# A tree layer's matmuls in another order, and an alignment's planned lengths

## The chip, the core and the metric

The kernel runs on one core of a Trainium2 chip. The metric is the device time of one execution in microseconds, as the median of several runs. The profile comes from one further execution.

## The reference

A decoder of four layers works on 64 sequences of 64 tokens with 128 features, and a context of the same shape. Each layer adds an attention, a cross part and a feed-forward part to the tokens `x`. Two parts of the first layer matter here.

The cross part of the first layer is an alignment: for each sequence, the distances between its context rows and its tokens, the cheapest path through the 64x64 table, found by running sums over rows and then followed back, and the context rows added to the tokens along that path.

The feed-forward part of the first layer has three decision trees (`q`, `k`, `v`) of 16 leaves. Each token falls into one leaf of each tree and goes through that leaf's small two-layer network; then tokens attend to each other inside a sequence:

```python
sel = one_hot(leaf, 16)
hidden_all = relu(einsum('nd,ldh->lnh', xf, w1) + b1[:, None, :])
hidden = hidden_all * sel.T[:, :, None]
out = einsum('lnh,lho->no', hidden, w2) + sel @ b2
```

## The kernel before

The 4096 tokens form 8 blocks of 512. The work is written as small parts. A part has a name, a function that issues its instructions, the engines that may run it with a planned length on each, the parts it must follow, and the buffers it takes and frees. `Flow.add` (line 124) collects parts. `Flow.search` (223) plays the list many times with random priorities, from planned lengths alone, and keeps the shortest play. `Flow.run` (263) then issues the parts in that order and fixes the order of instructions on every engine (`Pinned`, 66). There are three such plans: for the first layer (`L0_group`, 1183), for the second (`L1_group`), and for the third and fourth together (`L2_group`, 2303).

Every engine works through its own list in order, so a part that waits holds up what stands behind it on that engine. SP issues almost all loads and stores, also in order: first inputs and weights, then the zeroing of large DRAM buffers (lines 2300 and 1910), then the trees' weights (1493, 1495), then what the parts ask for.

The parts of the first layer, in the names that the text uses:

- Attention, per block: normalization (`bn`, `rs`, `xn`), transposes, keys and queries, key masks `m0` to `m3` (405 on VectorE, 403 on ScalarE), four score parts (466, 16 rows in the trace each), their row maxima (487) and subtractions (496) on VectorE, exponentials (501), transposes and their evictions (1063, 517), value parts (531), divisions (557 to 562), then a norm per head, whose sums are on VectorE (620, 632) and whose power and scaling are on GpSimd (1074, 639), projection and residual (664, 667).
- Distances, per block: a load of the context rows (1307, 1309), the part `aa` on ScalarE, which squares them (1314), products (1334, 1335), inverses and a Newton step on VectorE (1345 to 1351), and a store to DRAM.
- Alignment, for blocks 0 to 2 and for blocks 3 to 7: one load of the distances; parts `c0` to `c15` on VectorE, each four rows of running sums (1392, 1393); then per chunk of eight rows `k` (1413 to 1415) and `l` (1421 to 1423), which make masks, and `t15` down to `t0`, each four rows of the way back (1433 to 1438); then one store, and per block the path part: loads (1466, 1468), a product (1473) and an addition (1476).
- Trees, per block: decision `dc` on VectorE (1530 to 1548), a transpose of the choice and its evictions `lo` (1554 to 1563), which also makes the bf16 tile `notT` that is 1 for each leaf that was not chosen. For each of three trees, eight chunks of two leaves, taken in pairs: `u` (1565) makes a pair's hidden values in a two-bank PSUM buffer, `r` (1577) adds the bias and applies relu, one half after the other, mostly on ScalarE (1583), and `d` (1588) multiplies by the second weights (1599; for the third tree 1609, with the 16-row product 1611 for the leaves' biases). Then scores, a softmax and the sum of values.

A chunk of `u` has two matmuls into one PSUM bank. The large product (1573) multiplies the 128 features with a chunk's weights in float32, which the trace shows as two passes of 512 columns. The small one (1574) has 16 rows of bf16: it adds a huge negative number to the hidden values of all leaves that a token did not choose, so that relu makes them zero. Large and small products alternate: chunk 0 large, chunk 0 small, chunk 1 large, chunk 1 small. There are two such PSUM buffers for `u` and for the attention's scores together.

Of the kernel before, what the change touches and what calls it, by code (L numbers as in the profile page):

```python
# [24 lines left out]
S = 64  # L25
# [30 lines left out]
CH = 8  # L56
# [47 lines left out]
class Flow:  # L104
# [19 lines left out]
    def add(self, key, on, f, after=(), takes=(), frees=(), shift=0.0, late=False, tail=0.0):  # L124


        assert key not in self.keys, key
        self.keys.add(key)
        ring = lambda n: RING.get(n, n)
        need = {}  # L130
        for n, _, _ in takes:
            r = ring(n)
            k, room = need.get(r, (0, 0))
            need[r] = k + 1, max(room, k + 1, ROOM.get(n, 0))
        self.wait.append((key, on, f, tuple(k for k in after if k is not None), [(ring(n), n, t, u) for n, t, u in takes],
                          [(ring(n), t) for n, t in frees], shift, late, tail, [(r, k, room) for r, (k, room) in need.items()]))
# [832 lines left out]
class Decoder:  # L969
# [321 lines left out]
    def flow_L0_xattn(self, fl, blks, p0, x):  # L1291

        nc, g = self.nc, blks[0]
# [78 lines left out]
        def add(name, on, f, after=(), takes=(), frees=(), tail=0.0):  # L1372
            fl.add(G(name), on, f, after=[G(a) if isinstance(a, str) else a for a in after],
                   takes=[(r, G(t), u) for r, t, u in takes], frees=[(r, G(t)) for r, t in frees], tail=tail)
# [29 lines left out]
        def least(c):  # L1404
            def f(e):
                t = self.sb("mk", (P, CH * (3 * S + 1)), BF16)
                du = t[:, 0 : CH * 2 * S].rearrange("p (i a j) -> p i a j", a=2, j=S)
                lf = t[:, CH * 2 * S :].rearrange("p (i j) -> p i j", j=S + 1)
                mk[c] = du, lf
                a, b = slice(CH * c, CH * c + CH), slice(CH * c + 1, CH * c + CH + 1)  # L1410
                cd, cu, cl = r[sl, a, 0:S], r[sl, a, 1 : S + 1], r[sl, b, 0:S]
                mn = self.sb("mn", (P, CH, S))
                nc.vector.tensor_tensor(mn[sl], cu, cl, ALU.min)
                nc.vector.tensor_tensor(du[sl, :, 0], cd, mn[sl], ALU.is_le)
                nc.vector.tensor_tensor(du[sl, :, 1], cu, cl, ALU.is_le)
            return f

        def back(c):
            def f(e):
                du, lf = mk[c]  # L1420
                nc.vector.memset(lf[sl, :, S : S + 1], 0.0)
                nc.vector.scalar_tensor_tensor(du[sl, :, 1], du[sl, :, 0], 0.5, du[sl, :, 1], ALU.is_lt, ALU.mult)
                nc.vector.scalar_tensor_tensor(lf[sl, :, 0:S], du[sl, :, 0], 0.5, du[sl, :, 1], ALU.is_lt, ALU.subtract)
            return f

        def trace(k):

            def f(e):
                for i in range(4 * k + 3, 4 * k - 1, -1):
                    src = self.dt_en  # L1430
                    if i < S - 1:
                        st = self.dt_st
                        nc.vector.tensor_tensor(
                            st[sl, :, 0:S], self.bc(r[sl, i + 2 : i + 3, 1:], [n8, 2, S]), mk[(i + 1) // CH][0][sl, (i + 1) % CH], ALU.mult,
                        )
                        src = self.dt2.tile([P, S], F32, name="m")
                        nc.vector.tensor_tensor(src[sl], st[sl, 0, 1 : S + 1], st[sl, 1, 0:S], ALU.add)
                    nc.vector.tensor_tensor_scan(
                        r[sl, i + 1, 1:][:, ::-1], mk[i // CH][1][sl, i % CH, 1 : S + 1][:, ::-1], src[sl, ::-1], 0.0, ALU.mult, ALU.add,
                    )  # L1440
            return f

        per = CH // 4
        for c in range(S // CH - 1, -1, -1):
            add(f"k{c}", {"DVE": 1.8}, least(c), [f"k{c+1}"] if c < S // CH - 1 else [f"c{S//4-1}"],
                [("mk", f"m{c}", per + (c > 0)), ("mn", f"n{c}", 1)], [("mn", f"n{c}")])
            add(f"l{c}", {"DVE": 1.3}, back(c), [f"k{c}"])
            for k in range(per * c + per - 1, per * c - 1, -1):
                first = k == per * c + per - 1 and c < S // CH - 1
                add(f"t{k}", {"DVE": 3.0}, trace(k), [f"l{c}"] + ([f"t{k+1}"] if k < S // 4 - 1 else []), [],  # L1450
                    [("mk", f"m{c}")] + ([("mk", f"m{c+1}")] if first else []))

        def store(e):
# [54 lines left out]
    def flow_L0_ffn(self, fl, blk, x):  # L1508
        nc, one, c = self.nc, self.f0, self.c
        w1, w2, em, b2 = self.f0_w1, self.f0_w2, self.f0_em, self.f0_b2  # L1510
        st, xb = {}, self.x[blk]
        add, K = self.adder(fl, "L0_ffn", blk)
# [52 lines left out]
        def up(m, pr):  # L1565
            k = slice(32 * m, 32 * m + 16)

            def f(e):
                st["hT", m, pr] = self.sb("hT", (P, 2, BT))
                ps = st["up", m, pr] = self.pair()  # L1570
                for i in range(2):
                    ch = 2 * pr + i
                    nc.tensor.matmul(ps[:, i], w1[:, m, ch, :], st["xT"], start=True, stop=False)  # L1573
                    nc.tensor.matmul(ps[:, i], em[k, ch, :], st["notT"][k], start=False, stop=True)  # L1574
            return f

        def relu(m, pr):
            def f(e):
                ps, hT = st.pop(("up", m, pr)), st["hT", m, pr]
                for i in range(2):  # L1580
                    b = self.f0_b1[:, m, 2 * pr + i : 2 * pr + i + 1]
                    if e is nc.scalar:
                        nc.scalar.activation(hT[:, i], ps[:, i], AF.Relu, bias=b)  # L1583
                    else:
                        nc.vector.tensor_scalar(hT[:, i], ps[:, i], b, 0.0, ALU.add, ALU.max)
            return f

        def down(m, pr):
            k = slice(32 * m, 32 * m + 16)

            def f(e):
                if pr == 0:
                    st["dn", m] = self.acc([P, BT])
                    st["o", m] = self.sb("va" if m == 2 else "qk")
                ps, hT = st["dn", m], st.pop(("hT", m, pr))
                last = pr == 3
                if m < 2:
                    for i in range(2):
                        nc.tensor.matmul(ps, w2[:, m, 2 * pr + i, :], hT[:, i], start=(pr + i == 0), stop=False)  # L1599
                    if last:  # L1600
                        nc.tensor.matmul(ps, b2[k, :], st["selT"][k], start=False, stop=True)
                else:
                    if pr == 0:

                        nc.tensor.matmul(ps, self.onesb[0:1, :], em[0:1, 1:5, :].rearrange("p c f -> p (c f)"), start=True, stop=False)
                    for t in range(TB):
                        tok = slice(t * P, (t + 1) * P)
                        for i in range(2):
                            nc.tensor.matmul(ps[:, tok], hT[:, i, tok], w2[:, m, 2 * pr + i, :], start=False, stop=False)  # L1609
                        if last:  # L1610
                            nc.tensor.matmul(ps[:, tok], st["selT"][k, tok], b2[k, :], start=False, stop=t == TB - 1)
            return f
# [54 lines left out]
        add("lo", {"ACT": 1.15, "DVE": 1.35}, leaves_out, ["lv"], [], [("tp", "lv")])  # L1667
        for m in range(3):
            for pr in range(4):
                add(f"u{m}{pr}", {"PE": 2.15}, up(m, pr), ["xT", "lo"] + ([f"u{m}{pr-1}"] if pr else []), [("mm", f"u{m}{pr}", 1), ("hT", f"h{m}{pr}", 1)] + ([] if pr else [("dnq", f"d{m}", 1)]),  # L1670
                    [("xT", "xT"), ("nT", "nT")])
                add(f"r{m}{pr}", {"ACT": 1.4, "DVE": 1.5}, relu(m, pr), [f"u{m}{pr}"], [], [("mm", f"u{m}{pr}")])
                add(f"d{m}{pr}", {"PE": 1.75 + (pr == 3) * (.86 if m < 2 else .5)}, down(m, pr),
                    [f"r{m}{pr}"] + ([f"d{m}{pr-1}"] if pr else []),
                    [] if pr else [("av", f"d{m}", 1), ("va" if m == 2 else "qk", f"o{m}", 1)],
                    [("hT", f"h{m}{pr}")] + ([("selT", "selT")] if pr == 3 else []))
            add(f"o{m}", {"ACT": .65, "DVE": .72} if m else {"ACT": .65}, out(m), [f"d{m}3"], [], [("av", f"d{m}"), ("dnq", f"d{m}")])
# [909 lines left out]
```

## Time and profile before

| what | us |
|---|---|
| median of 3 runs | 2339.93 (2337.36 to 2343.73) |
| the profiled execution | 2339.11 |
| its span | 2336.9 |
| TensorE busy | 2002.4 |
| VectorE busy | 1335.8 |
| ScalarE busy | 1088.6 |
| GpSimd busy | 833.2 |
| line 1573, large products, 384 rows | 213.3 |
| line 1574, small products, 192 rows | 74.0 |

The span runs from the first to the last instruction of the core, so 2.2 us of the execution lie around it. The mean granted TensorE clock was 0.904. A row such as "x384" counts passes: a float32 matmul shows as two. Ends of matmuls are modelled and overlap the next start, so the start of one matmul to the start of the next says what it took. In the rows of waits, the columns are who waited, for whom, the sum, the number of times and the longest. In a timeline, the columns are start, length, engine, line, operation and tiles, shapes, and how many alike were merged.

### The profile page before, as it was taken

Reading aid. Unit: us, or ns where it says so; the run is one execution under the profiler, and the core shown is the slowest. Engines: PE = TensorE matmul, PEld = TensorE weight load, DVE = VectorE, ACT = ScalarE, POOL = GpSimd, SP = SyncE. Lnnn points to the kernel's source line nnn. Section 1 sums busy time; section 2 is a strip of 40 time slices with the busy share of each in tenths; the row PEclk is TensorE's granted clock in tenths of the full one; section 3 lists DMA queues with packets and bytes.
Section 4 is the critical chain, followed back from the end, with each engine's and each line's share of the span. In section 5 each row is a group of like instructions: output and inputs, shape, how many; then the busy total and the mean of one; then the engine's idle time right before and its main releaser. Section 6 shows DMA issues by size and latency. Waiting matters only on the chain.

```text
span 2336.9 us, 42116 instructions
## 1 busy us (share of the span) xinstructions
PE 2002.4 (86%) x16746; PEld 1296.9 (55%) x16746; DVE 1335.8 (57%) x3680; ACT 1088.6 (47%) x2111; POOL 833.2 (36%) x1157
## 2 busy tenths in 40 slices
PE   7570959999999999979699994899999998983995
PEld 4450643445353457756476762566776765662763
DVE  8489887974020027967712333878978776871121
ACT  6560433233232347755323332666757765651432
POOL 7410460002000016453721116862235334143776
PEclk9785569999999999988799995899999999986998
DMA  9310021011000000000224441100000000012543
GB/s 255 94 37 5 19 71 23 1 25 27 0 1 0 1 10 2 15 27 16 64 74 132 139 156 44 33 10 2 6 6 25 2 6 20 6 37 79 93 80 29
DMA packets 146769, 97.78 MB, mean 42 GB/s; under 512 B 36477, under 2 KB 137646, under 8 KB 146318
## 3 DMA queue, kind: packets, MB, share of 16 engines
q1 hardware_dynamic: 125598, 63.39, 10.5%
q0 software_dynamic: 20976, 31.72, 5.7%
q8 instruction: 132, 2.16, 0.4%
q14 instruction: 63, 0.52, 0.1%
HBM read 58.67 MB, written 36.40 MB: 41 GB/s over the span
## 4 chain that ended last, share of the span: by engine, by line
PE 57%; DVE 17%; POOL 13%; issue 5%; DMA 4%; SPq 3%; ACT 1%; POOLq 0%; DVEq 0%; ACTq 0%
PE mm L1573 8%; PE ps L1063 6%; PE ps L1599 5%; PE ps L531 5%; POOL out_x L2396 4%; PE mm L466 4%; PE mm L2020 4%; PE ps L2028 3%; PE ps L1609 3%; PE mm L1574 3%; DVE e L487 3%; DVE B L496 2%; POOL moe_x L834 2%; PE ps L421 2%; DMA out_x<-ye,to 2%
## 5 line engine op out<-in xcount | busy, mean ns | idle before, releaser
L466 PE MATMUL mm<-K,G 32*64 32x256 f32 x2560 | 175.3, 414 | 86.1 <-DVE B L496 82.6
L517 ACT COPY B<-ps 128x512 f32<-128x512 f32 x320 | 178.4, 587 | 116.4 <-PE ps L1063 115.3
L1583 ACT ACTIVATE H<-mm,f_b 128x512 f32<-128x512 f32 x182 | 115.2, 684 | 245.8 <-PE mm L1574 245.8
L501 ACT ACTIVATE B<-B 128x1024 f32<-128x1024 f32 x160 | 168.3, 1058 | 117.1 <-DVE B L496 116.0
L1573 PE MATMUL mm<-G,w 128*128 128x512 f32 x384 | 213.3, 638 | 0.0
L487 DVE TENSOR_REDUCE e<-mm 128x16 f32<-128x1024 f32 x160 | 193.4, 1216 | 29.8 <-PE mm L466 28.2
L531 PE MATMUL ps<-vx,B 128*64 128x18 f32 (+1 forms) x5120 | 182.5, 219 | 32.6 <-ACT B L517 26.9
L1063 PE MATMUL ps<-cpack,B 128*128 128x128 f32 x1280 | 196.6, 294 | 11.6 <-ACT B L517 5.7
L531 PEld LDWEIGHTS ps<-vx,B 128*64 128x64 f32 x5120 | 169.3, 143 | 66.3 <-ACT B L517 32.9
L496 DVE TENSOR_TENSOR B<-mm,e 128x1024 f32<-128x1024 f32 x160 | 192.4, 1215 | 3.5 <-PE ps L1063 0.7
L1063 PEld LDWEIGHTS ps<-cpack,B 128*128 128x128 f32 x1280 | 152.9, 149 | 60.4 <-issue 29.0
L1073 POOL TENSOR_SCALAR rs_t<-ln_mv 128x4 f32<-128x4 f32 x88 | 17.5, 199 | 470.1 <-DVE ln_mv L1144 426.9
L466 PEld LDWEIGHTS mm<-K,G 32*64 32x64 f32 x2560 | 83.7, 139 | 145.8 <-issue 100.0
L1063 PE MATMUL ps<-cpack,G 128*128 128x128 f32 x544 | 98.4, 304 | 68.4 <-ACT G L1164 30.5
L2396 POOL DMA_INDIRECT out_x<-ye,to x80 | 125.1, 1564 | 52.5 <-DVE ye L2394 28.2
L1631 DVE TENSOR_TENSOR G<-ps,cpack 128x512 f32<-128x512 f32 x8 | 5.5, 686 | 236.2 <-PE ps L1628 236.1
L1063 PEld LDWEIGHTS ps<-cpack,G 128*128 128x128 f32 x544 | 67.5, 151 | 104.6 <-ACT G L1164 39.2
L1164 ACT ACTIVATE G<-x,ln_sh,ln_rs 128x128 f32<-128x128 f32 x224 | 92.1, 485 | 66.1 <-POOL ln_sh L1158 66.1
L1599 PE MATMUL ps<-H,w 128*128 128x512 f32 x256 | 120.6, 608 | 0.0
L2021 ACT ACTIVATE hT<-mm,w 128x512 f32<-128x512 f32 x92 | 63.2, 687 | 121.7 <-PE mm L2020 106.4
L1574 PEld LDWEIGHTS <-f_em 16*128 16x128 bf16 x192 | 17.4, 90 | 146.7 <-issue 146.7
L2384 ACT ACTIVATE hT<-mm,f_b 128x512 f32<-128x512 f32 (+1 forms) x96 | 58.9, 616 | 84.0 <-PE mm L2383 83.5
(424 smaller groups left out, 4255.1 us busy)
## 6 DMA issues: line engine op xcount, KB each, us to landing
xe<-pages SPq DMA_DIRECT2D x23, 264.0 KB
paged<-ye SPq DMA_DIRECT2D x23, 256.0 KB, 2.4
pages<-z SPq DMA_DIRECT2D x11, 528.0 KB, 10.2
moe_x<-z SPq DMA_DIRECT2D x8, 660.0 KB, 9.2
xe<-moe_x SPq DMA_DIRECT2D x8, 660.0 KB
G<-in_ctx SPq DMA_DIRECT2D x16, 256.0 KB, 3.1
ctxT<-in_ctxT SPq DMA_DIRECT2D x2, 2048.0 KB, 9.1
w<-in_L_ffn_w SPq DMA_DIRECT2D x16, 256.0 KB, 3.3
```

The source lines that it names most:

```text
L466: nc.tensor.matmul(sc[b * S : (b + 1) * S, gi, pr * 256 : (pr + 1) * 256], qT[rows, at : at + S], kx[rows, :, at : at + S], start=self.bia ...
L487: nc.vector.tensor_reduce(mx, sc.rearrange("p g (r k) -> p (g r) k", k=S), AX.X, ALU.max)
L496: nc.vector.tensor_tensor(ex, sv, d.bc(st["mx", u].unsqueeze(2), [P, 16, S]), ALU.subtract)
L501: nc.scalar.activation(st["ex", u], st["ex", u], AF.Exp)
L517: (nc.scalar.copy if e is nc.scalar else nc.vector.tensor_copy)(st["pT", u][:, gi], st.pop(("pt", u, gi)))
L531: nc.tensor.matmul(av[b * S : (b + 1) * S, pr, 2 * gi + jp], pT[:, gi, 2 * pr + jp, b * S : (b + 1) * S], v[:, (2 * dp + pr) * 2 + b, 2 * ...
L1063: self.nc.tensor.transpose(t[:cols, i, :], src[:, i, :], self.ident)
L1573: nc.tensor.matmul(ps[:, i], w1[:, m, ch, :], st["xT"], start=True, stop=False)
L1583: nc.scalar.activation(hT[:, i], ps[:, i], AF.Relu, bias=b)
L1599: nc.tensor.matmul(ps, w2[:, m, 2 * pr + i, :], hT[:, i], start=(pr + i == 0), stop=False)
L2020: nc.tensor.matmul(ps, w[:, ch * P : (ch + 1) * P], q["xT"], start=True, stop=True)
L2396: d = nc.gpsimd.indirect_dma_start(self.out[:, :], bass.IndirectOffsetOnAxis(ap=to[:, r0 + i : r0 + i + 1], axis=0), ye[:, r0 + i, :], Non ...
```

## The change

In `u`, a pair has both large products first and both small ones after them; before, each chunk had its large and its small product together. The number of matmuls, their operands and their PSUM banks are the same.

Four planned lengths change: those of the alignment's parts `k`, `l` and `t` on VectorE, and that of `u` on TensorE. The instructions of these parts are the same apart from the order inside `u`; the plan of the first layer is searched with the new lengths.

```diff
-            add(f"k{c}", {"DVE": 1.8}, least(c), [f"k{c+1}"] if c < S // CH - 1 else [f"c{S//4-1}"],
+            add(f"k{c}", {"DVE": 2.1}, least(c), [f"k{c+1}"] if c < S // CH - 1 else [f"c{S//4-1}"],
                 [("mk", f"m{c}", per + (c > 0)), ("mn", f"n{c}", 1)], [("mn", f"n{c}")])
-            add(f"l{c}", {"DVE": 1.3}, back(c), [f"k{c}"])
+            add(f"l{c}", {"DVE": 1.75}, back(c), [f"k{c}"])
...
-                add(f"t{k}", {"DVE": 3.0}, trace(k), [f"l{c}"] + ([f"t{k+1}"] if k < S // 4 - 1 else []), [],
+                add(f"t{k}", {"DVE": 3.35}, trace(k), [f"l{c}"] + ([f"t{k+1}"] if k < S // 4 - 1 else []), [],
...
                 for i in range(2):
-                    ch = 2 * pr + i
-                    nc.tensor.matmul(ps[:, i], w1[:, m, ch, :], st["xT"], start=True, stop=False)
-                    nc.tensor.matmul(ps[:, i], em[k, ch, :], st["notT"][k], start=False, stop=True)
+                    nc.tensor.matmul(ps[:, i], w1[:, m, 2 * pr + i, :], st["xT"], start=True, stop=False)
+                for i in range(2):
+                    nc.tensor.matmul(ps[:, i], em[k, 2 * pr + i, :], st["notT"][k], start=False, stop=True)
...
-                add(f"u{m}{pr}", {"PE": 2.15}, up(m, pr), ["xT", "lo"] + ([f"u{m}{pr-1}"] if pr else []), [("mm", f"u{m}{pr}", 1), ("hT", f"h{m}{pr}", 1)] + ([] if pr else [("dnq", f"d{m}", 1)]),
+                add(f"u{m}{pr}", {"PE": 2.35}, up(m, pr), ["xT", "lo"] + ([f"u{m}{pr-1}"] if pr else []), [("mm", f"u{m}{pr}", 1), ("hT", f"h{m}{pr}", 1)] + ([] if pr else [("dnq", f"d{m}", 1)]),
```

## The prediction

> **What bounds the kernel now.** I read the busy rows by slice first, to find where the two edited layers lie.
>
> ```profile
> PE   7570959999999999979699994899999998983995
> DVE  8489887974020027967712333878978776871121
> PEclk9785569999999999988799995899999999986998
> ```
>
> A slice is 58.4 us. TensorE is full from the seventh slice on, where the trace has the first large product of the trees (line 1573, 360.2 us), until the last of line 1611 at 864 us. Before that TensorE has holes and VectorE is the fuller engine. So the first layer has two stages with different limits. The busy time by stretch (TensorE, weight loads, VectorE, ScalarE, GpSimd, then the granted clock) says it in numbers:
>
> ```profile
> 60.00:80.00 20.00, 0.00 (x0) 0.00 (x0) 0.00 (x0) 1.70 (x9) 2.26 (x2) 0.50 0.94 221
> 80.00:100.00 20.00, 17.78 (x262) 16.09 (x264) 10.43 (x33) 14.65 (x31) 9.10 (x8) 0.81 0.10 33
> 220.00:240.00 20.00, 8.05 (x80) 5.94 (x82) 18.56 (x50) 3.41 (x5) 2.28 (x4) 0.50 0.00 1
> 600.00:620.00 20.00, 20.00 (x46) 6.73 (x46) 0.00 (x0) 6.33 (x10) 0.00 (x0) 1.00 0.01 1
> ```
>
> Two holes lie before 360 us. The waits of ScalarE (40 to 100 us) and of TensorE (160 to 240 us) name them:
>
> ```profile
> ACT G L1314 <- DMA G<-in_ctx: 31.0, 1, 31.0
> ```
> ```profile
> PE mm L466 <- DVE B L496: 67.8, 1, 67.8
> ```
>
> The first: ScalarE reaches the alignment's squares (part `aa`) at 47.3 us and waits until 78.3 us for a load that SP issues only at 75.67 us, behind its zeroing and weight loads. VectorE runs dry at 57.6 us and resumes at 83.0. The second is VectorE doing the first alignment alone, from 158 to 230 us.
>
> In the tree stage TensorE alone decides. Its timeline there:
>
> ```profile
> 600.66 1.13 PE L1573 MATMUL mm<-G,w 128*128 128x512 f32 x2
> 601.72 0.38 PE L1574 MATMUL mm<-nT,f_em 16*128 16x512 bf16 x1
> 602.04 1.12 PE L1573 MATMUL mm<-G,w 128*128 128x512 f32 x2
> 603.10 0.38 PE L1574 MATMUL mm<-nT,f_em 16*128 16x512 bf16 x1
> 603.41 3.70 PE L1599 MATMUL ps<-H,w 128*128 128x512 f32 x8
> 606.95 1.02 PE L1573 MATMUL mm<-G,w 128*128 128x512 f32 x2
> 607.90 0.38 PE L1574 MATMUL mm<-nT,f_em 16*128 16x512 bf16 x1
> ```
>
> Starts count here, since ends are modelled. A chunk (large product in two passes, small one in one) takes 602.04-600.66 = 1.38 us, a pair 603.41-600.66 = 2.75. Eight large passes in a row take 606.95-603.41 = 3.54: 0.53 for the first after a small product, 0.43 for each of the other seven. A large product that follows a large one takes 607.90-606.95 = 0.95 before its small one starts; one that follows a small one takes 1.06.
>
> **The trees' edit.** From these starts: a large pass next to large passes is 0.43; before a small product the last is 0.95-0.43 = 0.52 (+0.09); after a small product the first is 0.53 (+0.10). A small product before a large one takes 0.31. Its second cost is unseen before: the first of two small products in a row, with the same 16 rows and other weights. The nearest row is line 1611, two passes in 16 rows and 128 columns:
>
> ```profile
> 519.07 0.48 PE L1611 MATMUL ps<-b,G 16*128 16x128 f32 x2
> 519.48 0.71 PE L1609 MATMUL ps<-w,H 128*128 128x128 f32 x4
> ```
>
> The two passes last 519.48-519.07 = 0.41 us. Their starts are 0.21 and 0.20 apart; a plain pass of 128 columns is 0.11, so each has one extra of about 0.1, as for entering and for leaving the 16 rows, and the load between them is hidden. A small tree product of 0.31 likewise holds 0.21 of streaming (half a large pass) and one extra 0.1. So two of them cost 0.21+0.31 with the load hidden, or 0.31+0.31 with it bare.
>
> New pair: 0.53+0.43+0.43+0.52+0.21+0.31 = 2.44, against 2.75: 0.30 saved (0.09 into the mask, 0.10 in the mask, 0.10 out of it, once per pair). There are 96 pairs (192 rows of line 1574 by two), all after 360 us: 96 x 0.30 = 28.9 us. Bounds: 31 us if both extras of the mask vanish in places, 19.3 us if the load is bare (pair 2.54).
>
> Here the Trainium skill speaks against the change. *TensorE: Matmul & The Clock Gate*, section "The mechanism", says that a weight load overlaps matmuls in flight only if it goes to another row group. Both masks of a pair share a row group, and so do the large products: by that rule masks cost 0.31+0.31, and large passes should not run at 0.43 either (a clause before it leaves room for a background weight buffer, without saying when that serves). The row of eight passes with eight loads at 0.43 contradicts it for the large ones, line 1611 for 16 rows. I take 28.9 and keep 19.3 as a rival. *TensorEngine Tiling (Array Packing)*, "Key Properties", says that changing the tiling mode drains TensorE; the +0.09 before each small product fits that, and it is what the edit halves.
>
> Evictions: `relu` of the first half now starts after the first mask, when both large products are done. The two halves take 0.69 each (line 1583, 684 ns), so they end about 1.05 us after the pair instead of 0.7. The next pair that needs this buffer comes a whole pair later (2.44 us), so 1.4 us of slack are left; ScalarE is busy 6.3 of 20 us there. Value 0; if a softmax part sits in front (4 instructions, some 2 us), up to 0.6 us, for 24 such parts and normalizations at most 10 us. I take 1 us.
>
> **The lengths.** They change no instruction; they make the planner choose another order in the first layer. The order of the changed program shows: the second and third layer group are untouched apart from a few shifted normalizations; in the first group each engine's row list changes. Before the first large product stand the same 1464 TensorE and 796 VectorE instructions as before. What differs is where they stand to the two waits.
>
> (a) The squares. ScalarE has 46 parts before its first `aa` now, 37 in the new order. SP's list up to that load is the same, so it still arrives at 78.3 us. Work standing behind the wait grows. VectorE stops at the first key mask of block 0 (its key follows `aa` on ScalarE): it will have done 8 maxima and 8 subtractions instead of 12 and 11, and one key mask less: 4x1.216+3x1.215+0.545 = 9.1 us. TensorE stops at a transpose of block 2, with 40 parts done instead of 49: four score parts, four transposes, one value part fewer, 4x1.91+4x0.5+1.9 = 11.5 us. Both engines were near full from 83 to 158 us, so the start of the first alignment moves from 158 to about 168: +10 us. Bounds: 0 (the longer queue closes the 15 us of VectorE gaps in that stretch), 11.5.
>
> (b) From there to the first large product VectorE is the limit again. Of its work some 2 us more lie in the stretch by part counts (masks and one eviction that ScalarE had). Attention resumes in the second hole at part `t11` rather than `t9`, with the same two pairs of PSUM. Value +2, bounds -6 to +6.
>
> (c) The tail: at present the last head norm's sums (line 632) stand before the alignment's last rows, now after them. That puts its 5.5 us power, projection and residual 11 us after the alignment's end instead of 8; the path's own store and loads already take 10 to 11.5. Also the 2 MB load of the context and the next layer's weights stand nearer the path's store on SP: four small loads between store and path loads hide in the 5.4 us wait for the store. Value +2, bounds 0 to +8.
>
> (d) The second alignment must be ready when the first three blocks' trees end. Now its last row is at 507.9, its first product could run at about 520, and TensorE asks at 531.2. In the new order TensorE asks 11.5 us earlier relative to its first large product (35 pairs x 0.30 and slightly other parts), and the alignment starts 2 us earlier: cover of 11 falls to about 2. Value +1, bounds 0 to +6.
>
> Sum: -28.9 + 1 + 10 + 2 + 2 + 1 = -13 us. The profiled execution took 2339.11 us (span 2336.9 and 2.2 around), so 2326; the median of the runs, 2339.93, is 0.8 above it and gives 2327. I write 2326.
>
> **The rivals.**
>
> A. The mask's load is bare (the skill's rule). Then -19.3 + 16 = -3: 2336. For it: the two masks share their rows. Against: line 1611.
>
> B. Slower: TensorE comes back from the longer first hole at half clock and stays there. Place: 80 to 168 us, where some 82 us of TensorE time (72.5 busy from 80 to 160, times 101/90 for the backlog) were at a mean clock of 0.87. The rows show 0.50 in a hole and 0.81 right after it. At a mean of 0.65 the same work takes 82x0.87/0.65 = 110, +28 us: 2354. It decides from a clock of about 0.7 down, where it eats 20 us. Against: the hole of 26 us already gave 0.81 at once, and it grows by about 10.
>
> C. The order costs nothing: (a) is swallowed by the gaps, as VectorE is idle 15 of 75 us there, and earlier resumption in the second hole pays for the tail. Then 2339 - 28 = 2311.
>
> **The numbers.** Forecast 48%, A 17%, B 17%, C 18%. Within 0.3% (7 us, about what a measurement of this kernel can tell) means 2333 to 2347. Forecast: 42 faster, 6 same. A: 3, 11, 3 slower. B: 2 same, 15 slower. C: 18 faster. Together 0.63, 0.19, 0.18. The range reaches from below C (the 31 us bound, 2304) into B (2350); the forecast's own is 2317 to 2335.
>
> **What would show it.** Right, if starts in the tree stage give 2.44 us per pair and the first to last large product shrinks from 497 to about 470 us; if ScalarE waits some 36 to 40 us for the squares' load; if the first large product starts near 374 us. Wrong, if a pair takes 2.54 (A), if the clock from 80 to 168 us is below 0.7 (B), if the first large product starts at 362 or earlier (C), or if TensorE waits long at the second alignment's products (line 1473) or evictions hold pairs back.

## The result, and the profile after

The changed kernel takes 2335.17 us (median of 20 runs, 2325.43 to 2339.00), the kernel before 2339.50 (20 runs, 2333.48 to 2343.73). The ratio is 0.9979, with an interval of 0.9969 to 0.9989: faster by 4 us, where 14 were forecast. On a second chip the ratio was 0.9967 (0.9954 to 0.9980). The profiled execution of the changed kernel took 2338.67 us, with a span of 2336.9, the same as before. Its rows by slice:

```profile
PE   6581737999999999969799985899999998973995
DVE  6389896994102037968513334877878776871121
PEclk9686568999999999989799995899999999986998
```

TensorE is full from the eighth slice on, and the slices ahead of that are emptier: VectorE starts with 6, 3 where before it had 8, 4, and the clock of the second slice is 6 instead of 7. The same stretches as before show why (columns as before):

```profile
60.00:80.00 20.00, 0.00 (x0) 0.00 (x0) 0.00 (x0) 1.58 (x9) 1.09 (x2) 0.50 0.99 219
80.00:100.00 20.00, 19.00 (x161) 14.12 (x162) 9.61 (x18) 8.86 (x20) 3.01 (x4) 0.50 0.03 10
220.00:240.00 20.00, 0.00 (x0) 0.00 (x0) 18.52 (x56) 0.00 (x0) 5.69 (x5) 0.50 0.04 14
600.00:620.00 20.00, 20.00 (x101) 11.99 (x101) 1.55 (x3) 7.29 (x17) 0.00 (x0) 1.00 0.00 1
```

From 80 to 100 us TensorE is busy for 19.00 us but gets through 161 instructions, at a granted clock of 0.50; before it did 262 in 17.78 us at 0.81. The two waits that name the holes (of ScalarE from 20 to 100 us, of TensorE from 160 to 260) are now:

```profile
ACT G L1314 <- DMA G<-in_ctx: 29.7, 1, 29.7
```
```profile
PE ps L1063 <- POOL G L639: 58.9, 1, 58.9
```

In the tree stage the new order is seen at once:

```profile
600.91 1.99 PE L1572 MATMUL mm<-G,w 128*128 128x512 f32 x4
602.83 0.60 PE L1574 MATMUL mm<-nT,f_em 16*128 16x512 bf16 x2
603.36 1.98 PE L1572 MATMUL mm<-G,w 128*128 128x512 f32 x4
605.27 0.60 PE L1574 MATMUL mm<-nT,f_em 16*128 16x512 bf16 x2
605.80 1.98 PE L1572 MATMUL mm<-G,w 128*128 128x512 f32 x4
```

A pair takes 603.36-600.91 = 2.45 us, the next 605.80-603.36 = 2.44. It was 2.75.

For all kernels that follow, the span can be cut at five places: the end of the wait for the squares' load, the first alignment's first row, its last row, the first large product, and the last product of line 1609. The column "load at" below is the time of the first of these, and each column behind it but the last is the length of one stretch in us, read from the trace of one execution. The first six rows are the two kernels themselves, profiled several times in the runs below.

| execution | load at | to first row | alignment | to first large | trees | from there to the end | span |
|---|---|---|---|---|---|---|---|
| before | 78.3 | 79.7 | 174.9 | 27.3 | 503.7 | 1472.9 | 2336.8 |
| before, second | 77.7 | 79.2 | 172.3 | 28.6 | 503.3 | 1473.3 | 2334.4 |
| changed | 78.4 | 95.0 | 176.3 | 31.9 | 474.3 | 1480.9 | 2336.8 |
| changed, second | 82.2 | 94.1 | 175.5 | 31.9 | 474.2 | 1486.2 | 2344.1 |
| changed, third | 79.1 | 93.7 | 174.4 | 31.8 | 476.1 | 1472.7 | 2327.8 |
| changed, fourth | 78.0 | 88.6 | 176.2 | 32.0 | 473.7 | 1478.3 | 2326.8 |
| e1, pair alone | 82.0 | 78.8 | 172.8 | 28.5 | 477.9 | 1550.4 | 2390.4 |
| e2, lengths alone | 81.6 | 88.2 | 173.9 | 31.8 | 503.5 | 1554.1 | 2433.1 |
| e3, changed, early load | 48.7 | 90.8 | 176.3 | 32.0 | 474.1 | 1556.9 | 2378.8 |
| e4, before, early load | 47.2 | 94.0 | 175.1 | 27.1 | 505.5 | 1555.8 | 2404.7 |
| e5, wide mask | 77.8 | 78.9 | 172.6 | 28.3 | 461.6 | 1480.7 | 2299.9 |
| e7, pair, early load | 48.4 | 94.4 | 170.4 | 28.7 | 475.4 | 1471.5 | 2288.8 |
| e8, pair and its length | 84.4 | 84.7 | 157.4 | 37.9 | 484.7 | 1475.2 | 2324.3 |
| e9, pair, VectorE lengths | 84.2 | 74.8 | 178.9 | 28.6 | 474.3 | 1468.6 | 2309.4 |

Between the first and the third row, the trees give 503.7-474.3 = 29.4 us. Of these, 15.3 are lost again ahead of the alignment, 1.4 in it and 4.6 behind it. At the end of the trees 8.0 us are left, and the last 8 go in layers whose order of parts the change hardly touches.

My theory after this (T1): the pair's order is worth 29 us whatever the plan; the lengths made another plan, which costs some 20 us of it, in two places: the work behind the squares' wait, and the stretch from the alignment's last row to the first large product. The rivals: T2, denser TensorE work itself brings more half-clock stretches in later layers, so part of the gain is given back whatever the plan; T3, the pair's order pays only with lengths that fit it.

### The profile page after: what moved, and what is told of

Same layout as the page of the kernel before. It is cut to its first block, busy times and chain, and to the rows that moved or that the text cites. A ratio compares the mean times of both kernels' runs of the same rounds, so it can differ in the third digit from the quotient of the medians.

```text
span 2336.9 us, 42144 instructions
## 1 busy us (share of the span) xinstructions
PE 1979.5 (85%) x16746; PEld 1302.6 (56%) x16746; DVE 1338.5 (57%) x3685; ACT 1083.7 (46%) x2101; POOL 832.9 (36%) x1162
## 3 DMA queue, kind: packets, MB, share of 16 engines
q8 instruction: 132, 2.16, 0.4%
## 4 chain that ended last, share of the span: by engine, by line
PE 59%; DVE 15%; POOL 14%; issue 5%; DMA 3%; SPq 2%; ACT 2%; POOLq 0%; DVEq 0%; ACTq 0%
PE mm L1572 8%; PE ps L1063 7%; PE ps L531 5%; PE ps L1599 5%; PE mm L466 5%; POOL out_x L2396 5%; PE mm L2020 4%; PE ps L2028 3%; PE ps L1609 3%; PE mm L1574 2%; POOL A L2090 2%; DVE e L487 2%; PE ps L421 2%; PE ps L373 2%; DVE B L496 2%
## 5 line engine op out<-in xcount | busy, mean ns | idle before, releaser
L1063 PE MATMUL ps<-cpack,B 128*128 128x128 f32 x1280 | 203.8, 302 | 43.7 <-ACT B L501 30.4
L1063 PEld LDWEIGHTS ps<-cpack,B 128*128 128x128 f32 x1280 | 159.5, 154 | 94.5 <-ACT B L501 39.3
L1572 PE MATMUL mm<-G,w 128*128 128x512 f32 x384 | 187.6, 611 | 0.0
L2396 POOL DMA_INDIRECT out_x<-ye,to x80 | 125.0, 1563 | 53.0 <-DVE ye L2394 28.7
L466 PEld LDWEIGHTS mm<-K,G 32*64 32x64 f32 x2560 | 84.0, 142 | 78.8 <-issue 36.7
L1572 PEld LDWEIGHTS mm<-G,w 128*128 128x128 f32 x384 | 67.6, 191 | 81.4 <-issue 80.9
L2384 ACT ACTIVATE hT<-mm,f_b 128x512 f32<-128x512 f32 (+1 forms) x96 | 58.9, 616 | 84.8 <-PE mm L2383 84.4
```

The costliest lines, as they stand in the source:

```text
L466: nc.tensor.matmul(sc[b * S : (b + 1) * S, gi, pr * 256 : (pr + 1) * 256], qT[rows, at : at + S], kx[rows, :, at : at + S], start=self.bia ...
L1063: self.nc.tensor.transpose(t[:cols, i, :], src[:, i, :], self.ident)
L1572: nc.tensor.matmul(ps[:, i], w1[:, m, 2 * pr + i, :], st["xT"], start=True, stop=False)
L2396: d = nc.gpsimd.indirect_dma_start(self.out[:, :], bass.IndirectOffsetOnAxis(ap=to[:, r0 + i : r0 + i + 1], axis=0), ye[:, r0 + i, :], Non ...
```

## The experiments

e1 to e4 ran on a chip on which every kernel was slower; the kernel before took 2422.13 us there (11 runs). Only times of one chip are compared.

**e1, the pair alone.** The changed kernel with the four lengths of before:

```diff
-            add(f"k{c}", {"DVE": 2.1}, ...
+            add(f"k{c}", {"DVE": 1.8}, ...
```

and likewise 1.3 for `l`, 3.0 for `t`, 2.15 for `u`.

> The pair's new order of products alone, with the four planned lengths of before, so that the planner's order of parts is that of before. T1 (the trees' edit is worth 29 us whatever the plan; what the changed kernel lost, it lost through the new plan): first alignment's first row at 158 us and first large product at about 360 us as before, a pair 2.44 us, the first layer's last tree product some 28 us earlier than before, time about 2311. T2 (denser TensorE work brings more half-clock stretches later, so part of the gain is given back at the clock whatever the plan): same first layer, but the later layers longer by 7 to 10 us, 2318 to 2322. T3 (the pair's order only pays with the lengths that fit it): 2330 or more, with idle TensorE between pairs or at the second alignment.

Measured: 2391.11 us, 0.9875 of before (0.9851 to 0.9899), 31 us less. First row and first large product stand where before has them (160.8 and 362.1 us, with the load 3.7 us later than in the profile of before). The interval leaves a gain of 24 to 36 us, which is more than T2's 17 to 21 and than the 9 at most of T3. The tree stage itself is 25.6 us shorter than in e2 on the same chip (477.9 against 503.5): here TensorE waits 1.8 us for the second alignment's path load (line 1473), and 3.4 us at half clock follow, which cost 1.7.

**e2, the lengths alone.** The kernel before with the four new lengths, so the changed kernel's order of parts with the old order in the pair.

> The four planned lengths alone, with the pair's order of products of before: the order of parts is that of the changed kernel. T1: the new plan costs 15.5 us at the squares' wait (first alignment's first row at 173 us) and 4 to 6 us between the alignment's last row and the first large product, which starts at 381 us; a pair stays at 2.75; time about 2360. T2: the plan costs only what the first layer shows and some 7 us less than the whole loss of the changed kernel, so also about 2360 but with unchanged later layers. T3 (lengths are harmless without the pair's order): 2340.

Measured: 2446.67 us, 1.0118 of before (1.0089 to 1.0146), 24.5 us more by the medians and 22 to 35 by the interval. This speaks against T3. By the medians of e1 and e2 both edits together would be 6 us less, about what the changed kernel is; with intervals of some 6 us on each, they agree with it but do not prove that nothing else is at work. The table shows one price as forecast and one not: 31.8 us to the first large product, as in the changed kernel, but 88.2 us from the load to the first row, 9.4 more than e1, where the changed kernel has 95.0. The two stand in the same order here, so the first 20 us after the hole can be laid side by side. TensorE in the changed kernel:

```profile
80.69 1.11 PE L1063 MATMUL ps<-cpack,B 128*128 128x128 f32 x4 [26.89 <-ACT B L501]
82.11 2.82 PE L1063 MATMUL ps<-cpack,B 128*128 128x128 f32 x12 [0.30 <-ACT G L386]
...
86.72 1.98 PE L466 MATMUL mm<-K,G 32*64 32x256 f32 x16
```

and in e2:

```profile
83.86 1.11 PE L1063 MATMUL ps<-cpack,B 128*128 128x128 f32 x4 [29.99 <-ACT B L501]
85.28 2.82 PE L1063 MATMUL ps<-cpack,B 128*128 128x128 f32 x12 [0.30 <-ACT G L386]
...
89.11 1.09 PE L466 MATMUL mm<-K,G 32*64 32x256 f32 x16
```

The first two rows, transposes, take the same time in both. Of the rows behind them, one is shown: e2 needs 1.09 us for a score part and the changed kernel 1.98. So in e2 the full clock is back 4 us after the hole, in the changed kernel's execution after 20.

**e3 and e4, the wait taken away.** In the changed kernel (e3) and in the kernel before (e4), SP zeroes the large buffers later, so that the squares' load is not behind that:

```diff
-            if "L3_ffn" in layers:
-                self.setup_L3_ffn()
-            if "L1_ffn" in layers:
-                self.setup_L1_ffn()
+            self.loads = 0
...
                 nc.sync.dma_start(st["cT"], self.ins["ctxT"][:, blk * BT : (blk + 1) * BT])
+                self.loads += 1
+                if self.loads == 2:
+                    self.setup_L3_ffn()
+                    self.setup_L1_ffn()
```

> The changed kernel, with the zeroing and weight loads of the feed-forward layers issued on SP behind the second context load of the distances instead of ahead of the first, so the load that the squares wait for lands before ScalarE comes to them. T1 (10 to 15 us of the changed kernel's loss stand behind that wait): no long wait of ScalarE, TensorE and VectorE without the 27 us hole near 55 to 82 us, and against the next run the two plans start the first alignment within about 3 us of each other; time about 2335 less 27 to 38, some 2300. If the plan's loss had nothing to do with the wait, the 15 us between the two plans stay here: some 2312.

> The kernel before, with the same early context load. T1: the hole of about 25 us goes, the first alignment starts some 20 to 25 us earlier, time about 2316; the changed kernel with the same edit is then faster than this one by about 22 to 25 us instead of 4. If the wait is not what parts the plans, that difference stays near 4 to 10 us.

Measured: e3 2388.10 us, 0.9866 (0.9841 to 0.9890); e4 2402.43, 0.9906 (0.9878 to 0.9934). In the traces, T1's place is confirmed: with the load early the alignment starts at 139.5 us in e3 and 141.2 in e4, so the new plan's 15 us are gone, and the stretch behind the alignment keeps its 4.9 (32.0 against 27.1). At the end of the trees the two stand 27 us apart (821.9 and 848.9), and the rest takes the same time. But these are e3's fastest execution and e4's slowest. The medians differ by 14, between T1's 22 and the 4 to 10 of the other reading, and with intervals of some 6 us on each they decide for neither. The totals leave T1 open; the stretches in the traces bear it out for the place ahead of the alignment.

**The changed kernel on another chip, and half of the lengths each.** The next four runs shared a chip (before: 2343.59 us, 12 runs).

> The changed kernel once more, on the chip of the next three runs. If the net gain of 4 us holds on another chip: 0.997 to 0.999 of the kernel before. On the chip of the four runs ahead of this the edits taken singly were -31 and +24.5 us; if they simply add, 6 us less than the kernel before, 0.997. T2 (the gain is given back at the clock in later layers): little more than nothing, 1.000.

Measured: 2337.89 us, 0.9967 (0.9954 to 0.9980), 5.7 less. That is what the medians of the two single edits add up to, and against T2.

e8 has the pair's order with the new length of `u` and the old ones of `k`, `l` and `t`; e9 the reverse.

> The pair's order and the new planned length of the large pair (2.35), with the three VectorE lengths of before. It gives a third order of parts: ScalarE has 48 rows ahead of the first squares (48 before, 40 in the changed kernel), but a head norm's sums stand behind the alignment's last row as in the changed kernel. T1 (two places of the order cost time: the rows ahead of the squares' wait, and the head norm behind the alignment): first alignment near 160 us, 5 us lost between its end and the first large product, so some 23 us less than before, 2316 where before is 2339, ratio 0.990. If the plan's loss sits in the wait alone: 28 less, 0.988. If any departure from the old order costs as much: 4 to 8 less, 0.997.

> The pair's order and the three new VectorE lengths, with the old planned length of the large pair (2.15). ScalarE has 50 rows ahead of the first squares, and no head norm stands behind the alignment's last row. T1: neither of the two places costs, so the whole 28 us stay: 2311 where before is 2339, ratio 0.988. If the VectorE lengths as such carry the loss: 4 to 8 less, 0.997.

Measured: e8 2324.69 us, 0.9915 (0.9901 to 0.9929), 19 less; e9 2322.42, 0.9914 (0.9897 to 0.9932), 21 less. So neither kind of length carries the loss by itself. e8 loses 37.9-27.3 = 10.6 us in the stretch behind the alignment, where 5 were forecast: its path load is issued later and TensorE waits 9.7 us for it. Its first row also comes 84.7 us behind the load, 5 later than in before, though as many rows of ScalarE stand ahead of the squares. Its alignment took only 157.4. Its trees took 10 us more than the changed kernel's; 10.2 us at half clock in them cost half of that, and they hold 52 rows of TensorE more (1767 against 1715), 32 of them of lines 1334 and 1335, which stand elsewhere in the other plans. e9's profiled execution shows what T1 forecast: 74.8 us to the first row, 28.6 to the first large product, 474.3 for the trees, a span 27 us below that of before. It is e9's fastest execution; the median, 21 us less than before, is 6 us short of that.

**e7, pair and early load.** e1 with the edit of e4.

> The pair's order with the four lengths of before and the early context load: the two things that singly gave -31 and -20 us on the chip of the runs ahead. If they add, -51 us there, ratio 0.979 (2290 where before is 2339); if a later wait, that at the second alignment above all, eats part of it, 0.982 to 0.987.

Measured: 2291.05 us, 0.9783 (0.9762 to 0.9805), 52.5 us less than before. The two gains add, and next to nothing of them is lost at the second alignment (0.8 us of wait there). This version is faster than both kernels.

**e5, a mask over 96 rows.** The kernel before, with the small product over the rows of all three trees:

```diff
-                    nc.tensor.matmul(ps[:, i], em[k, ch, :], st["notT"][k], start=False, stop=True)
+                    nc.tensor.matmul(ps[:, i], em[:, ch, :], st["notT"], start=False, stop=True)
...
-    for t in range(3):
+    for t in range(1):
```

The second edit leaves only the first tree's pattern in the constant, so this kernel leaves out the masks that the second and third tree need.

> The kernel before, with the small masking product over 96 rows instead of 16. Its constant holds the pattern of the first tree only, so all three trees are masked by the first tree's leaf: this part of the computation is changed. It asks what the extra 0.1 us ahead of, in and behind each small product is. If it is the change of the rows in use (128 to 16 and back): a large product takes 0.43 + 0.43 everywhere and a small one 0.21, a pair 2.14 instead of 2.75, 96 x 0.61 = 58 us less TensorE time, of which some 10 us come back as a wait at the second alignment: about 2291 where before is 2339. If it is the other type (float32 and bfloat16 in turn): no change, 2339. A use of 96 rows out of 128 may also count as a change of rows: then 2339 too.

Measured: 2305.62 us, 0.9860 (0.9830 to 0.9891). The order within a pair is the old one, yet:

```profile
600.46 1.02 PE L1573 MATMUL mm<-G,w 128*128 128x512 f32 x2
601.32 0.38 PE L1574 MATMUL mm<-nT,f_em 96*128 96x512 bf16 x1
601.54 3.60 PE L1599 MATMUL ps<-H,w 128*128 128x512 f32 x8
```

A chunk takes 601.54-600.46 = 1.08 us instead of 1.38, so a pair 2.16: the large product 0.86 with no extra on either side, the small one 0.22. The types alternate as before, so the number of rows in use makes the extra time, not the type. Of the 57.6 us (192 chunks by 0.30) the tree stage shows 503.7-461.6 = 42.1. TensorE is without a product in it for 5.3 us more than before (6.2 against 0.9), mostly in two waits of 1.6 and 4.1 us, the second for the second alignment's path load. Behind each of these it runs at half clock, for 3.4 and 6.8 us, which costs 5.1. The other 5 us are not traced.

**Three more profiles,** on a third chip, to see which losses stay.

> The changed kernel, profiled once more, to see which of its losses stay from one execution to the next. The two profiles up to here had TensorE at a granted clock of 0.50 for 20 us after its first long hole (before: 6 us), and half-clock stretches between 1520 and 1800 us, where before has none. T1 with the clock as a matter of chance: in some execution the first lasts 4 to 8 us, the first alignment then starts 9 us later than before instead of 15, and a total of 2326 to 2330 goes with it. T2 (the changed plan has them always): 0.50 for 20 us again, and 7 us or more lost between 1520 and 1840 us again.

> As the run before this one: a further profile of the changed kernel. Under chance, the length of the half-clock stretch after the first hole and the losses between 1520 and 1840 us differ from those of the other profiles; under T2 they are the same.

> The kernel before, profiled a second time, for the same question from the other side. If the plan decides the clock: again no half-clock stretch between 1520 and 1840 us and some 6 us at half clock after the first hole. Under chance: a loss of some us in one or the other place.

Measured: 2329.68, 2328.66 and 2336.67 us. The question has two answers. For the first stretch, from the end of TensorE's first hole to the alignment's first row, here is before, then the changed kernel as first profiled, then its fourth profile:

```profile
81.00:158.00 77.00, 70.52 (x945) 53.33 (x946) 58.88 (x123) 61.23 (x121) 33.05 (x37) 0.87 0.13 31
```
```profile
80.70:173.40 92.70, 83.62 (x1058) 62.55 (x1066) 69.40 (x146) 64.55 (x125) 40.85 (x42) 0.80 0.12 27
```
```profile
80.20:166.60 86.40, 76.06 (x1060) 57.48 (x1068) 69.05 (x147) 64.69 (x125) 41.05 (x42) 0.88 0.12 29
```

The last two rows are the same order of parts: 1058 and 1060 TensorE instructions, 146 and 147 of VectorE, where before has 945 and 123. At the clock of before (0.88 against 0.87), the extra work costs 86.40-77.00 = 9.4 us; at 0.80 it costs 15.7. So the clock there is a matter of the single execution, the backlog is the plan's.

The later layers answer otherwise. Between 1520 and 1840 us all four profiles of the changed kernel have a half-clock stretch of 10.2 us, which begins 2 to 3 us behind an idle of 0.84 us ahead of a score part. All other traces have that idle too, but of these only e5, which keeps the plan of before, has such a stretch behind it; e2 and e3, which have the changed kernel's plan, have none. So the plan alone does not decide it, and T2 as put is wrong.

The clock records of the traces say more. The granted clock in them is either 1.00 or 0.50. In all 14 traces every half-clock stretch but the last, which the end of the span cuts, lasts a whole number of 3.41 us (3.41, 6.83, 10.24 and so on), and all of one trace begin on one grid of that step. The grid lies differently against the work in each execution. Here is the step in which the idle falls and what follows it, for before (second profile) and the changed kernel (fourth):

```profile
1621.12:1624.53 3.41, 2.57 (x21) 1.75 (x23) 3.34 (x4) 3.00 (x5) 0.13 (x1) 1.00 0.00 0
1624.53:1627.95 3.42, 3.42 (x66) 2.33 (x59) 2.85 (x5) 3.42 (x12) 0.00 (x0) 1.00 0.02 5
```
```profile
1612.77:1616.18 3.41, 2.57 (x53) 1.89 (x51) 2.98 (x3) 3.00 (x8) 0.00 (x0) 1.00 0.02 5
1616.18:1626.42 10.24, 10.24 (x82) 6.29 (x79) 7.32 (x15) 4.21 (x12) 0.00 (x0) 0.50 0.01 2
```

TensorE is busy for 2.57 us of that step in both. But in before the step holds the wide products of line 2118 (384 columns) ahead of the idle, in the changed kernel the small score and value products behind it. The place on the grid parts all 14 traces: in the nine without a stretch the idle begins 1.95 to 3.07 us into a step, in the five with one between 0.17 us ahead of a border and 0.52 behind it. No run moved the grid or the idle by itself, so this is a sign without exception and not a test. Why all four profiles of the changed kernel fell on the costly side is not shown.

The 20 us behind the first hole fit the same picture. Here is the first step behind the hole in the fourth profile of the changed kernel, then the first two in its first profile:

```profile
80.18:83.60 3.42, 3.06 (x13) 2.66 (x14) 1.67 (x4) 2.97 (x6) 0.00 (x0) 0.50 0.02 9
```
```profile
80.48:83.90 3.42, 2.90 (x13) 2.51 (x14) 1.67 (x4) 3.12 (x6) 0.00 (x0) 0.50 0.03 10
83.90:87.31 3.41, 3.41 (x45) 2.83 (x47) 0.44 (x2) 2.36 (x4) 0.00 (x0) 0.50 0.00 0
```

In the fourth profile this step holds 3.06 us of transposes, and the full clock is back at its end. In the first profile the grid begins 0.2 us ahead of the work instead of 0.06, the step holds 2.90 us of them, and the half clock goes on. TensorE is then busy without a break in four more steps, mostly with score and value parts, and the full clock is back only behind a fifth with projection and transposes (97.55 to 100.97). So what a step holds counts there, and not only how long TensorE is busy in it. What it must hold is not measured here.

## Why the prediction was off

The direction was right; the sum of -13 met -4.3. The trees' edit was right. The step that failed is what the order of parts costs at the clock that TensorE is granted: the sum put 10 us for the squares' wait at an unchanged clock and nothing for all that stands behind the trees, and the profiles have 13.4 and 6.4 in their place. A smaller miss is the tail, 4.0 for 2. By the sum's own terms, from the means of four profiles of the changed kernel and two of before:

- **The trees' edit, evictions and second cover** (-28.9, +1, +1): measured -28.9 for the whole tree stage (474.6 against 503.5). The steps of 2.44 us per pair are as worked out. The mask's load is hidden: the second of two masks starts 0.23 us after the first, and a pair is 0.10 below rival A's 2.54. So rival A fell, and with it, for this case, the rule that the Trainium skill has in *TensorE: Matmul & The Clock Gate*, "The mechanism", as far as that goes by the row group. Evictions and the second alignment cost nothing that shows in the changed kernel. That the whole stage gives the figure of the first term to the tenth is luck: in e1 the same edit gave 25.6 us there. From the first large product to the last it is 463 us where about 470 was forecast, but from the start of that last one 11.3 us follow to the end of line 1609, where before has 7.0.
- **(a) The squares' wait** (+10): measured +13.4 (92.9 against 79.5). This is the first term that was mis-sized. The order itself costs 9 to 9.4, as estimated, shown by the fourth profile and by e2 against e1, and it goes when the wait goes (e3 against e4). The rest is the clock. I named that mechanism as rival B, but only as all or nothing: to a mean of 0.65 or not at all. It came in part, to 0.80 in the first profile, and took 6 us there, which put the term beyond its bound of 11.5. *TensorE: Matmul & The Clock Gate*, "What's actually happening", gives about 3.4 us of sustained work until the full clock is back. By that a resumption would cost some 2 us (an estimate, half of that time); the nine traces with such a hole and another outcome have 3 to 8 us, and the first two of the changed kernel 20, with TensorE idle for no more than 0.3 us at a time. One sign that I gave for this step was wrong: ScalarE did not wait 36 to 40 us, but 29.7, since it reached the squares no earlier. The backlog was the right measure (8 row maxima done at that point where before had 12, as forecast), the wait was not.
- **(b) Up to the alignment's last row** (+2): measured +2.0.
- **(c) The tail** (+2): measured +4.0 (31.9 against 27.9), the second mis-sized term; e2 and e3 have it too, so it is the plan's. I counted the last head norm's chain, which now stands behind the last row:

```profile
349.89 0.65 DVE L632 TENSOR_REDUCE hn_vs<-G 128x32 f32<-128x512 f32 x1
...
361.68 0.69 DVE L667 TENSOR_TENSOR x<-x,ps 128x512 f32<-128x512 f32 x1 [8.27 <-PE ps L664]
```

The residual starts 11.8 us behind the sums, and the first path product (line 1473) 11.7 us behind the last row where before had 10.1, near the forecast. What I did not count comes after that. In both orders the decision products of three blocks (line 1526) stand ahead of the first large product, but in another order. Before, then the changed kernel:

```profile
353.05 1.98 PE L1526 MATMUL ps<-f_nw,G 128*128 128x45 f32 x16
...
358.48 1.94 PE L1526 MATMUL ps<-f_nw,G 128*128 128x45 f32 x8
360.21 1.20 PE L1573 MATMUL mm<-G,w 128*128 128x512 f32 x1
```
```profile
372.12 1.09 PE L1526 MATMUL ps<-f_nw,G 128*128 128x45 f32 x8
...
375.66 0.61 PE L1063 MATMUL ps<-cpack,sel 128*96 128x128 f32 x4 [2.00 <-DVE sel L1548]
...
378.37 3.48 PE L1526 MATMUL ps<-f_nw,G 128*128 128x45 f32 x16
381.64 1.20 PE L1572 MATMUL mm<-G,w 128*128 128x512 f32 x1
```

From the first of them to the first large product before takes 360.21-353.05 = 7.2 us, the changed kernel 381.64-372.12 = 9.5. In the new order TensorE waits 2.0 us for a choice (`sel`) that VectorE makes, which it did not have to wait for in the old one. And the last decision products, which run at half clock in both, are now those of two blocks: 3.27 us for 16 rows, where before has 1.73 for 8.

- **Everything behind the trees** (0, not a term at all): measured +6.4 (1479.5 against 1473.1), nearly all of it behind 1510 us, at the clock. The half-clock stretch of 10.2 us behind the idle of 0.84 us is in all four profiles and costs some 5 of it. Hardly an instruction moved there, so the sum put nothing; in truth the same instructions fell differently on the grid of the clock. This is the largest single miss. That the place on the grid goes with the stretch is seen in all 14 traces; why the changed kernel kept falling on the costly side stays open, and its four values (1472.7 to 1486.2) spread over more than the miss itself.
- **The load** came 1.4 us later on average (79.4 against 78.0), which is within what the executions of one kernel show.

Together -28.9+13.4+2.0+4.0+6.4+1.4 = -1.7 us for the mean of these profiles; the timed runs have -4.3 and -5.7, with executions of the changed kernel from 2325 to 2346 us. Rival C, that the order costs nothing, fell with e2.

## What to carry to other kernels

Cost an edit and the plan it triggers apart, and try them apart: here, on one chip, the edit alone was worth 31 us and the new lengths cost 24.5; on another, the edit with two other mixes of lengths was still worth 19 and 21. The new lengths lie nearer to the trace (a part `t` takes 3.4 us, a pair of `u` now 2.44) and gave the worse plan. A new length is worth taking only if the plan that it gives is. And work that a plan puts behind a fixed wait is paid for on the far side (9 of the 10 us estimated here), at whatever clock TensorE has after the hole. So shorten the wait first: the early load gave 20 us, and took away what the other plan cost ahead of the alignment.

## What the runs showed of the hardware

- A product over 16 rows between products over 128 costs about 0.1 us going in, and again coming out; two in a row pay it once (a pair of chunks takes 2.44 us instead of 2.75). With 96 rows it costs nothing (0.22 us for 512 bf16 columns between float32 passes). *TensorEngine Tiling (Array Packing)*, "Key Properties", has a drain at a change of tiling mode; here only the steps between 128 and 16 show one.
- After a hole of 20 to 30 us, the same products came back to the full clock after about 3, 4, 6 and 20 us (twice) in executions of the same order of parts. The half clock always lasted a whole number of 3.41 us, and an idle of 0.84 us was followed by 10.2 us of it or by none, with its place on that grid.
- A product of a single row can run along with one of 16 rows: in the changed kernel one of line 1605 starts 0.01 us behind a mask (607.73 and 607.72), and the next mask starts 0.23 us behind the first, as it does where nothing stands between them.
